# Deformable convolution and attention on one core: one transfer for a tile's places, and row maxima by way of DRAM

## The chip, the cores and the metric

The kernel runs on one core of a Trainium2 chip. The metric is the device time of one execution in microseconds. Three runs of the kernel before took 3164.89, 3168.13 and 3178.74 us; their median is 3168.13 us.

## What is computed

The input x is 8 images of 56 x 56 places with 128 channels, float32. Layer 0 is a block with a deformable 3 x 3 convolution, layer 1 causal attention over the 3136 places of an image and an expert layer in which each expert takes 8 places of each image.

```python
xp = x @ w_in + b_in
h = gelu(batch_norm(depthwise_conv3x3(x)))
offset, mask = h @ w_off + b_off, softmax(h @ w_msk + b_msk)   # 4 groups, 9 taps each
y = dcn_core(xp, offset, mask) @ w_out + b_out
x = x + gamma1 * layer_norm(y)
x = x + gamma2 * layer_norm(gelu(x @ w_fc1 + b_fc1) @ w_fc2 + b_fc2)
t = t + attention(norm(t))          # causal, softmax(q k / sqrt(T)) v, T = 3136
t = t + experts(norm(t))            # 64 experts, the 8 places of an image with the highest gate
```

`dcn_core` reads xp, padded by one place with zeros on each side, at nine shifted positions by bilinear interpolation. As long as no offset exceeds one place, each output place depends on the 5 x 5 places around it, and the interpolation becomes a sum over 25 taps with weights by place and group; places outside the image count as zero.

## The kernel before, in words

The work is cut into 32 groups: 8 images b with 4 groups s each. A group has one or two chunks of 448 places (8 rows of 56), that is 448 or 896 places, in tiles of up to 128: 200 tiles in all (`sizes`, `tiles`, lines 45 to 60).

For each group there are generators, each a step in the list `ORDER` (one letter a step, written out by hand or by a planner ahead of time): the program is laid down in exactly that order, and every engine works its own instructions off in the order in which they stand. A `need(...)` names an engine, an assumed duration, a buffer that is taken or given back, and from when; these figures do nothing in the program, they are what the order was planned with.

- `prepare` (L487): loads a chunk of x, transposes it on PE (L497), stores the transposed chunk to DRAM for later (`xTd`, L504), multiplies by `w_in` (L516) and stores the result into an image in DRAM (`img`, L529), in two transfers of 56 partitions. There are two such images, used in turn. An image has rows of `IW` = 60 places: 56 and two zero places on either side, with two zero rows above and below; the zeros are written once at the start (L347 to L354).
- `conv` (L538) and `plan` (L569): the depthwise convolution on DVE (L554), then offsets and masks, and from them on POOL the tap weights `taps` [128 places, tile, 5, 5 x 4 groups] (L631 to L645).
- `fetch` (L653): for each tile of 128 places, SP brings for each place its 5 x 5 x 128 values, 5 pieces of 640 values, into a buffer `g` of 3200 values a partition; three buffers exist. As a row of the image is 60 long and only 56 count, a tile's places are taken row by row of the image: 3 or 4 transfers with 8 to 56 partitions, 616 in all (L667).
- `weigh` (L673): DVE multiplies `g` by the weights (L692). `sums` (L697): POOL adds up the 25 parts in six additions (L708 to L718) into `ys`, after which the buffer is free for the next fetch.
- `project` (L778): output projection, norms and the two matrix products of the block on PE (L798, L812, L824), with norms on ACT, POOL and DVE.
- `norm` (L879): normalised places `z`, transposed `zT`, and the queries `qT`. Row 0 of `qT` is later used for the largest score, as `zT` holds a row of ones there.
- `scores` (L917) and `maxes` (L937): PE computes the scores of a tile of queries (L924), DVE takes the largest of each query (L947, L949) into `neg` [128 queries, tile], negated. The queries lie across partitions there, so at the end of a group PE transposes each column of `neg` into one row (L959, 224 in all) and ACT copies it into row 0 of `qT` (L966, 56 in all).
- `keyed` (L986), `exps` (L1006), `attend` (L1017): PE computes the scores once more with the keys across partitions and with the maxima already subtracted by row 0 (L993), ACT takes exponentials (L1014), PE multiplies by the values (L1025).
- `after` (L1040): residual, gate and the choice of the 8 places; at the end the experts' weights are loaded and the expert layer runs (`weights`, `hidden`, `share`).

The row that the change is about, and the fetch:

```python
for u in range(N // CH):                       # in maxes, L952
    pr = gen(f"pr{nm}_{u}")
    ...
    nc.tensor.transpose(pr[:1, ...], neg[r : r + w, i : i + 1], ident[r : r + w, r : r + w])
    ...
    nc.scalar.copy(qT[:1, u * CH : (u + 1) * CH], pr[:1, :CH])
while t < t0 + n:                              # in fetch, L662
    h0, w0 = divmod(t, HW)
    w = min(HW - w0, t0 + n - t)
    src = bass.AP(src.tensor, src.offset, [[C, w], [IW * C, 5], [1, 5 * C]])
    nc.sync.dma_start(g[t - t0 : t - t0 + w].rearrange("p (r f) -> p r f", r=5), src)
    t += w
```

SP issues the loads of x, the fetches, the loads of `xTd` and the weights, all in one queue in the order of `ORDER`; ACT issues the stores in its own.

Of the kernel before, what the change touches and what calls it, by code (L numbers as in the profile page):

```python
# [8 lines left out]
F32 = mybir.dt.float32  # L9
# [45 lines left out]
def tokens(b, s):  # L55
    return CH * sizes(b)[s]
# [18 lines left out]
def need(engine, us, take=None, give=None, since=None, kind=None, when=None, lock=False):  # L75
# [27 lines left out]
    "pppppppkbbpppwpwbpwwwppwpvkffvfvvvvvvvwvpbwpwccpcccpwcwcccppbccpcccwpcwpcpccvcwvcvcvcvcvcvcv"  # L103
    "cvwggvvvsvvwvwwvwvvsvgvpbpscsspsccsfpgppbpspcpscpscvscvssfvvcvcvcvcsvvcvscscsvcvcvcvvcvsvcfv"
    "cvcgvpbvpcccpvcvpvppbcvpcvcvsgpvgcsvccvscvvssvsvsfmvmpmvpvmvsvgvpbmpsmpscssmpsfmppbmpgmmpsmm"
    "pmmcsmpsmsvscvsfvcgcmscmcvgcsmcscsmsmsfvmkvmnnnnncsvnvvgsnnsnsnsnfcncgnnqcqqcqcxxcxxxcxctcte"
    "ctetaegaecaaccscagooccvsooovoosooscovvvsovsosfovovovovocosvpbopcsopscospsosfoppbpgcpsccosccs"
    "scsspfmpmvmgsmmvvsmvvssmsmsfmgmmsmmmmmsmsvvsssfmgmsmvvgmsmsmskmssfmgmmmmcmsmmsmcmmscmmscmgmm"
    "mscfcccmmcmcmcmcmkmnncnncnnncngcnsnnnccvcncvnvsnvnvgnsvnvnsnvsnsvsfvnvnpnbpqsqxqxqqsqsqsssfc"
    "xcxxxcqxccqxcqxcqqxqxxsqxqxqxsqxspxsgsxfmxmxxmtpstcptgvteetestmtacsaveavemaegsamsasttesfemea"  # L110
    "atmtaemceasvmmvvtsmvmsvtmsmssfamemgstvsmttgsmaeaesaessfaemgaamtctestmeaemakmcaammosmocmoscgm"
    "smcsmcfmomcmmcoocommocmmoomoomoocomccogomcoosmomomoccmokcsmvnnvnngsnnonnossovnovvovsonsfnvnv"
    "nvnnvnconsvononscponbpnsoossnsfvnvpnvcqpqxspvpqbxpqxqsxqxosqxsqcsxfxcmqmgqccqqmxsxqmxqxxqxqx"
    "sqcxqsxqxqsxsqxqsxmqfxcqmqxxqxqxqxcqcmqmcxcmxqxmmcxgcxmmcxpcmxmxpstmgtpmesvvsvamvtvtgessmtet"
    "esmtsftagaemeasmtemstkmasmesamssafemeamgttmetsmttaaesmeamsemssamsfmagamtettseaeteamcamcmcamc"
    "aemsgcsacmtsctemcegstcmsfcetcvcmamacesmaktmstcnncntsncnstncsntnscfaecepcabpagtnpeeetsntpntnt"
    "cnasnaecansnasesengsfanaeenanampnasmpnobpnosmncomcqoqxcoqocqxmxqxqxsqmxsqxssfmxqmqxomxqomocm"
    "oxcopgmmsqmmqcmpqcxpqxcvxqcxqvqxcqxocqgcqsmssxgssfxxxqmvqxqxmoqoqmxoqxqxxqsoxmoxqomoqsqxoxom"
    "sxoqksgosqmsfomqmmxqmxqsxqxqxmxqxqsxmqxsoxsmosqmsfoxmogqmmomsmoqmxmsxomvxsmvxsovssfvvxvxgctv"
    "stetstcvagsvtesvesavesfaevmavtoteooomttsectmgasmeasaesaesmafcvcmcakvcctgctmsemstmteevstcvpcs"  # L120
    "tbscmscpfsnannanenpnnnaeasgetmtstestpstaspsfpeabptagaepeseaaeaspatapststvsevtnfevaevgaemangn"
    "anstnntntnvenvtncvencaevnasveamagctsnesanssnsfmntmqeqxqxqxccqxcqxqcxacxcmcqmmxccqcmmsxgcmmst"
    "mstssccgsfmvccvevvcesvcavmavstvcmtvetvesmtstssfetcmgcaaecaesaevamacscpsqbpctsctsexpcfctpetge"
    "tpctcvtacaecvmevakvaecvaecmvcaaxamcxvomvxmoxctcmvocgtemteamatemeoaatmteameommoaoooaomomootmo"
    "motmemoootmtaomteoamomemoaomokmssonmonnmsnonenmsnonseosanofmoaaomnosmooommnonsmonnnosnmonsms"
    "gosnsfmmncnmnogmcnsonomoconosomvcvcsvscsvcsfvqvmoqxqxqxcmoqcqxsmqxqxcxqocxqxqcqsoxoxmsoxqsom"
    "sqofxomxqkmcomqcmqcomoxcqxmcxqxqxomxqovcmoxcvqocmxocmqovmvqmcxmxcogcxmmvcpmmbxmcxvmgcxpcopmo"
    "tptmoeottetgetptmaaevmeamvemakmsssssnpesntonsfntnbnptnanavepevnavpaevasnavnttnvptsteesaetsae"
    "stnsfnagntntenansgnanensansenssansfeaqqxqxsqxqxqxgmsqmqssmsfqmxsaxxtxtegaesaqqmxqxqsmxsqxqxs"
    "mxsqsfmqxmxgqmmscmmsccmxmvscqscmsqgcfsxcqxqxcqxcgptcbsctptscmescesescfcxcqmcqgttqmaaecqexmcx"  # L130
    "acxaxacmapmopcmocqkmqspnnqnnqnxqxqxnqxxqxsnqxnqxnxnqsxnxmsngpsmnbspsmfonxopxmxpsoqooqxoxcpqx"
    "cqovxqxoqcxqocqxomtxoxtesomtcagoeteqeqsoqsoxqsoxsfoqxoxqoqxoxoqxoqxgsvqxqvosvmoamssovsmvsofv"
    "amvavmxoxmmsgqomosmosqmsqossmfoxxxoosgtmqqseqmqxsxmqsxqsxstfxxtegcexvmsaavmaxsvgmvtkmscstesc"
    "tcfsvtcvtcveacgemamsemamsavtemvctvcstmcsctsecfacetcegtavcacacetctceaecpecmbpacmatcamepcmcmpc"
    "tgmmtmpmtmepmbpamaaemamtpeempampamtkmssvmesvtmvtsevtessvtsfvtvmvavaesaeaesaemasasstmftetsema"
    "gaetaesttetsetgmstmsasmesfagaeaeammsttamnosenntosasenosnensfmotmnonmaomngaeatsnaentoonstonoo"
    "tnosnotsonsaesfegcenanenanscgcnvcscacasvtscvstvsftvemevevnvcovvccgncsanoaoasoqoqcsmtsxxstcft"
    "omgetoaeeqeqvqxxqqmxqcacoomcaomcaxxmpkmxqcbgpcqocmoctmoxepcmcpoxcpocxvaovxovcxovtcxotceoaoot"
    "etvemavavemvtavemtatemeamatameommommotmomootomaoeomooaemtttemetmoaaameamemakmssonmnanmnonmsn"
    "onnosmostssftoetteoaoaeomaooonemonmannmonamnonnogcmnmonommnsccnmncvcmsnvcnomvcvmovovocosvsnv"  # L140
    "sqsfmvqvqxqvxqxoxpmqxbcoqxsmqxqxcomsxqcmgsqpsxqsxsqfovxqxmxpkmompqsmpmxopmscqbqxscqpsqxsmfxq"
    "xqxmqccmqmcxmcxqmxmocpxmcoxomcxgomxcomxomctcmoecgctmctctepcetgpmtaaeaevaevmavtvmetmvtemvtkms"
    "sssstvasnasefnnaennnaenanamomantotevtesnoaoenoaonsoaonotnsoonstonsesfnganentnnetsngneanoaaqs"
    "ooqxsoqxsosoqxsfoqxqoxoqxoqxoxtsogotsoesqeqsqxsxqsfxqxqxqxoxmosgomqqosmqxqsxmqxssxqsxfmxqmax"
    "mgamsmcmsmcgcsomsmvsctsfmcopeombgpsopsmqcspqsxqcmcxqxqcsxcfqxcqxmcqxqxpqcmtmtxexmetckmsssstc"
    "asagecaesacfaqqcaqxsqxqxxqxoxmcnxomspxmbnpgxcosxpmststnsnentmfeotenmgaoaseananmptnngopnocton"
    "otoeoenocootnceqmovgaaesoaoaoqosxoqxosvqosxoqsxosfqvqxqxoxmxovocmvcmvqvmqxsovqxqxcqvsqxoxmso"
    "xsgomsmsfotmqeqxqxsoqqxsxqoxqsooqssqsfxmxxgcqcmcsxqvcqmxcqxsmqxcasxvsxmcstmsfxvmxtvkmvtcevtc"
    "vstecvtevctsgcacsaegsmesamfaemecamgaamttteemaataemveamvacmcpcmmbtgcmcpmctctmmccpmcemcpcececp"
    "pabmaapmttepemapapmtvvtemtevmetvkmsssssvtsvtsfvtvavaetestaaesaesaesasesfattegttstaeaesaeaesg"  # L150
    "asasmasfmntnoennoamnnsnomntotsetgestestsftnoaoaeomgnaeaesnamttoeomnootseonotonansmnaesmesgas"
    "msfmcmnccnmvcocvnavnmnvsvanvonsvmnvosqqmvsqgvsqsfvgmooooosoxoxpxqbpsxqxqscmqxqxxqxcmptxspmst"
    "gftemetetpamvaevaevcavcvacvocmvtkocmocemoacmcoxogcmxcxmotxmtovtecvetcoetmcotocomamaectectaca"
    "ecaeaeaacmacmocmommommotomoomoooetmtttemaetmteomamemtkmssonmnoanamnnsonmennostesaostmnfoaaom"
    "eoetsoamoaooaemeanmansanmonosnonsnsmmngscsfnomnnccnvosgmncocmnsomncsocqososoqxsfqmxqxoqxqcgm"
    "cscvcsxxqsmvsqxsqfoomqoqxomxqxqxoxmoqmoqxomoxqxkmqxocmqmcomxoqcmxqcqomxqxcomxqcxomxqmocxmcvo"
    "xmcvmxvcmxvmxvomcmvtcmvtcgvmcvececgamcatmtoemovavometmomeakmssopooabmpsntnnstnsmnpnesseftptn"
    "pnptbpvmvnaveaevmavsavtteeansateantsesaesnasfgnantnntetemageasmnpnsmpnamnspsnsmnsfnmgmtnmqse"
    "qxqxsqxqsxqsxqsxsfqxqxqxqxqxsaxgmqsmmsqsmqsxsfmxxgscmqccmxqcqvsmcqcsxqcsxsqxsfxqcxmcxpcmqbcm"
    "xpqkscqxcmtsgtxectesctegctcttaaesasegsfaeaeaamqmqacnmsnnnonmqxnxqxoqsnqnxsnqxmqnxqxsmxqsxsfq"  # L160
    "xmxqmqgnmsnnpnsxmoxcqosxcqxpsoxcoqxxpxqxsqsfxqoxqqxxqoxmxcoqmocomxcoqmcoomqgcqcqcompmbpxxgxs"
    "oxogopmsqqomqpqxpsqxsvsxqmsxfqxqxoxoqxoqxosqvoxmomqosxmvoksmxsvmostvsfmoevtvtmgoeomsaaemoqva"
    "sxmqvstostesoootsftegaeceavsaacgscmvtxsmtesctsvsftveaveavecgaccasctctesteccmseacsmcmsvacfvmm"
    "cvamvcmcgtmcvcpmbpcccecpcmacpcxtpmtettgeeaaeatmtxpatbpatepeemptmptmtkmsssssssfvavaevtesvtasa"
    "etesvvvvsmvsasfaeaeaemttsgettstassgaesaesfaeaeagasttetseaeststeassfaeaatamnennnsomnnanntmtoe"
    "tengmoaaesnanstnosntsegtsfneoaenanmcmgsomccomsoomcsoaosvonosotvsfnvmmnvmmngtmotetmsovececosv"
    "oovsonvsasvcnfcgnctntctceacqecaqexacoxqecoqoxcqovcxqvqxqcxqxmcxqxpxabpmgacampcotopctecoctocm"
    "eomeaocmokmcomcamoptotovetetvotvvmvamvavaemveavmttetaemexmamexamaaxamxommotmmomtoemoooooeoam"
    "atmtteeaoamtatoemomtemoakmssonmnoannmsonenmnsonesomsanfaotomntetoooaseoeamnmnaomnanmsnnmmong"
    "csnmmsnsnsmmnsfcgcnmncvcmncvscvvvscvqmovqxoqqxcxoqvcqxcmqxxqsmxqsxsqxsfqxmxqvmqxmsqkxmvmqoxm"  # L170
    "cvmoxpcqboqmxcqxpqmxqcqmsxqxcvqxosxmsqxsmpcfxmooxmomcocooxcommxcommoxomtgcoetcmcecovvacmpacv"
    "ocpvpmvtbvtevmtoaeegmopaattmevmtkomssssssemsftnmgpettmasmpannoanseoenteompnaonaeosantmstosan"
# [2153 lines left out]
```

## Time and profile before

| | us |
|---|---|
| median of three runs | 3168.13 |
| profiled execution, device time | 3183.68 |
| its span in the trace | 3181.9 |
| TensorE (PE) busy | 2810.6 |
| GpSimd (POOL) busy | 2292.4 |
| VectorE (DVE) busy | 2210.9 |
| ScalarE (ACT) busy | 1629.2 |
| mean granted clock of PE | 0.94 of full |

In the trace's rows an instruction stands with its line, its engine, what it writes and reads (`g<-img` writes g from img), how many there were, their busy time in all, the mean duration in ns, and the idle time of the engine before them with what ended it. "PEld" is the loading of weights into TensorE, which goes beside matmuls. Each float32 matmul shows as two. The chain is followed back from the last instruction: at each step to what released it. A name ending in q is an engine's sequencer.

### The profile page before, as it was taken

Reading aid. Unit: us, or ns where it says so; the run is one execution under the profiler, and the core shown is the slowest. Engines: PE = TensorE matmul, PEld = TensorE weight load, DVE = VectorE, ACT = ScalarE, POOL = GpSimd, SP = SyncE. Lnnn points to the kernel's source line nnn. Section 1 sums busy time; section 2 is a strip of 40 time slices with the busy share of each in tenths; the row PEclk is TensorE's granted clock in tenths of the full one; section 3 lists DMA queues with packets and bytes.
Section 4 is the critical chain, followed back from the end, with each engine's and each line's share of the span. In section 5 each row is a group of like instructions: output and inputs, shape, how many; then the busy total and the mean of one; then the engine's idle time right before and its main releaser. Section 6 shows DMA issues by size and latency. Waiting matters only on the chain.

```text
span 3181.9 us, 37170 instructions
## 1 busy us (share of the span) xinstructions
PE 2810.6 (88%) x11785; PEld 1620.5 (51%) x11785; DVE 2210.9 (69%) x3887; ACT 1629.2 (51%) x3791; POOL 2292.4 (72%) x2415
## 2 busy tenths in 40 slices
PE   3458899999999999999998999998999999999671
PEld 3334455555555555555555555554555555655331
DVE  6766769777866896678668786687577855466540
ACT  2334565564666456664565556653666455633210
POOL 3878898778876898688858878677568885523543
PEclk7568899999999999999999999999999999999786
DMA  6866778647773787477845867467554857130360
GB/s 167 168 152 147 159 154 180 151 110 168 174 163 80 166 176 160 104 154 170 173 104 112 191 159 168 99 145 155 108 128 100 191 128 148 34 135 12 119 223 26
DMA packets 279862, 442.35 MB, mean 139 GB/s; under 512 B 18977, under 2 KB 132921, under 8 KB 279657
## 3 DMA queue, kind: packets, MB, share of 16 engines
q1 hardware_dynamic: 189352, 382.34, 54.7%
q10 hardware_dynamic: 87040, 51.40, 5.9%
q0 software_dynamic: 3264, 6.15, 0.7%
q8 instruction: 95, 1.56, 0.2%
q14 instruction: 111, 0.90, 0.1%
HBM read 386.03 MB, written 53.95 MB: 138 GB/s over the span
## 4 chain that ended last, share of the span: by engine, by line
PE 57%; DVE 14%; DMA 12%; POOL 9%; ACT 3%; issue 3%; SPq 1%; another core or an unknown queue 1%; ACTq 0%; POOLq 0%; DVEq 0%
PE sc L924 13%; PE av L1025 11%; PE st L993 11%; DMA g<-img 9%; PE ph L812 4%; DVE g L692 4%; PE pm L824 4%; POOL g L708 2%; DVE pv L554 2%; DMA xTd<-xc 2%; POOL g L710 1%; DVE mx L947 1%; PE py L798 1%; PE pg L1097 1%; PE pc L1054 1%
## 5 line engine op out<-in xcount | busy, mean ns | idle before, releaser
L692 DVE TENSOR_TENSOR g<-g,tp 128x3200 f32<-128x3200 f32 (+1 forms) x200 | 696.1, 3482 | 267.4 <-DMA g<-img 184.5
L708 POOL TENSOR_TENSOR g<-g 128x1536 f32<-128x1536 f32 (+1 forms) x200 | 688.9, 3445 | 60.2 <-DVE g L692 53.3
L924 PE MATMUL sc<-zT,qT 128*128 128x512 f32 (+4 forms) x1594 | 625.5, 525 | 18.1 <-DVE mx L947 8.2
L993 PE MATMUL st<-qT,zT 128*128 128x448 f32 (+8 forms) x1606 | 630.5, 513 | 10.2 <-ACT pe L1014 3.9
L1025 PE MATMUL av<-pe,zk 128*128 128x448 f32 (+8 forms) x1606 | 625.1, 513 | 16.3 <-ACT pe L1014 12.8
L1014 ACT ACTIVATE pe<-st 128x448 f32<-128x448 f32 (+8 forms) x803 | 392.1, 504 | 367.0 <-PE av L1025 175.6
L947 DVE TENSOR_REDUCE mx<-sc 128x1 f32<-128x512 f32 (+6 forms) x797 | 439.8, 583 | 97.4 <-PE sc L924 81.4
L924 PEld LDWEIGHTS sc<-zT,qT 128*128 128x128 f32 x1594 | 274.0, 188 | 266.2 <-issue 116.2
L1025 PEld LDWEIGHTS av<-pe,zk 128*128 128x128 f32 (+1 forms) x1606 | 286.3, 192 | 240.2 <-issue 166.2
L993 PEld LDWEIGHTS st<-qT,zT 128*128 128x128 f32 (+1 forms) x1606 | 278.1, 191 | 225.8 <-issue 155.9
L710 POOL TENSOR_TENSOR g<-g 128x768 f32<-128x768 f32 (+1 forms) x200 | 363.5, 1818 | 10.9
L554 DVE SCALAR_TENSOR_TENSOR pv<-xg,dw,pv 128x448 f32<-128x448 f32 x448 | 307.4, 686 | 31.0 <-ACT pv L551 19.8
L812 PE MATMUL ph<-xT,fc 128*128 128x512 f32 (+2 forms) x448 | 221.7, 586 | 24.9 <-DVE xT L754 21.8
L816 ACT ACTIVATE hid<-ph,b_fc 128x512 f32<-128x512 f32 (+2 forms) x224 | 140.8, 634 | 149.1 <-PE ph L812 146.8
L712 POOL TENSOR_TENSOR g<-g 128x384 f32<-128x384 f32 (+1 forms) x200 | 201.4, 1007 | 12.1
L645 POOL TENSOR_TENSOR taps<-taps,a 128x252 f32<-128x252 f32 (+1 forms) x288 | 190.5, 661 | 18.8
L635 POOL TENSOR_TENSOR a<-w 128x756 f32<-128x756 f32 (+1 forms) x96 | 135.8, 1415 | 86.2 <-DVE w L626 77.0
L824 PE MATMUL pm<-fc,hid 128*128 128x128 f32 x1600 | 194.7, 280 | 0.0
L824 PEld LDWEIGHTS pm<-fc,hid 128*128 128x128 f32 x1600 | 184.1, 193 | 11.6 <-issue 11.4
L1231 POOL TENSOR_TENSOR share<-share,part 128x512 f32<-128x512 f32 x56 | 71.0, 1268 | 130.8 <-DVE part L1221 114.0
L742 POOL TENSOR_SCALAR ssb<-ssb 128x4 f32<-128x4 f32 (+1 forms) x56 | 11.7, 208 | 176.3 <-ACT sqb L740 175.8
L812 PEld LDWEIGHTS ph<-xT,fc 128*128 128x128 f32 x448 | 78.4, 200 | 90.3 <-issue 41.1
(259 smaller groups left out, 4213.0 us busy)
## 6 DMA issues: line engine op xcount, KB each, us to landing
g<-img SPq DMA_DIRECT2D x280, 700.0 KB
g<-img SPq DMA_DIRECT2D x56, 600.0 KB
g<-img SPq DMA_DIRECT2D x56, 500.0 KB
g<-img SPq DMA_DIRECT2D x56, 400.0 KB
g<-img SPq DMA_DIRECT2D x56, 300.0 KB
w1t<-in_L_ffn_weight_dram SPq DMA_DIRECT2D x32, 512.0 KB
w2t<-in_L_ffn_weight_dram SPq DMA_DIRECT2D x32, 512.0 KB
xin<-in_x_dram SPq DMA_DIRECT2D x56, 224.0 KB
```

The costliest lines, as they stand in the source:

```text
L554: nc.vector.scalar_tensor_tensor(p3, src, dw[:, k : k + 1], p3, op0=ALU.mult, op1=ALU.add)
L692: nc.vector.tensor_mul(g3, g3, tp[:n, lt % 4].unsqueeze(2).to_broadcast([n, NTAP * NG, 32]))
L708: nc.gpsimd.tensor_add(g[:n, : 12 * C], g[:n, : 12 * C], g[:n, 12 * C : 24 * C])
L710: nc.gpsimd.tensor_add(g[:n, : 6 * C], g[:n, : 6 * C], g[:n, 6 * C : 12 * C])
L712: nc.gpsimd.tensor_add(g[:n, : 3 * C], g[:n, : 3 * C], g[:n, 3 * C : 6 * C])
L812: nc.tensor.matmul(ph[:, :n], fc1[:, f * P : (f + 1) * P], xT[:, :n], start=True, stop=True)
L824: nc.tensor.matmul(four(pm, m)[:, i, :], hid[:, f, i * P : (i + 1) * P], fc2[:, f, :], start=False, stop=i == m - 1 and f == 3,)
L924: nc.tensor.matmul(pp[:w, :n], qT[:, i * P : i * P + w], zTs[b, g][:, k0 : k0 + n], start=True, stop=not diagonal,)
L947: nc.vector.tensor_reduce(mx[:w, i, j : j + 1], pp[:w, :n], AX.X, ALU.max)
L993: nc.tensor.matmul(pp[:w, :n], zTs[b, g][:, j * P : j * P + w], qT[:, u * CH + q0 : (u + 1) * CH], start=True, stop=m <= 0,)
L1014: nc.scalar.activation(pe[:w, :n], pp[:w, :n], AF.Exp, scale=SCALE)
L1025: nc.tensor.matmul(av[:, q0:CH], zs[b, g][:w, j, :], pe[:w, : CH - q0], start=first, stop=last)
```

## The change

Three things are edited, and the order is written anew.

1. The image in DRAM loses its side borders: rows are 56 places long, with two places ahead of all and two behind. A tile's 128 places then stand 512 bytes apart throughout, across ends of rows, and `fetch` is one transfer of 128 (or 64) partitions x 5 x 640 values for each tile. A place near a side now reads places of the row above or below in the columns that lie outside.
2. These columns are masked: a constant `inside` [128, 7, 20], made from the column of each place, is 0 where a tap lies outside, and `plan` multiplies `taps` by it on POOL, once for each group. The columns come from an input that the general path already had.
3. `maxes` no longer transposes `neg`. ACT stores it to a row in DRAM (two such rows in turn), one value at a time; SP loads the row, of up to 896 values, into row 0 of `qT`. For a group of 448 places the store takes two transfers.

`ORDER` is another list of the same steps, planned with other figures for `need`, and a few small buffers share a tag.

```diff
-    imgs = [indram(f"img{j}", [IW * IW, C]) for j in range(2)]
+    imgs = [indram(f"img{j}", [IW * HW + 4, C]) for j in range(2)]
+    rows_ = [indram(f"maxes{j}", [GT * P]) for j in range(2)]
...
+    column = cst.tile([P, GT, 2], F32, tag="column", name="column")
+    nc.sync.dma_start(column, pos[:, :GT, :])
+    inside = cst.tile([P, GT, 5 * NG], F32, tag="inside", name="inside")
+    nc.vector.memset(inside, 1.0)
+    for k, limit, op in ((0, 2.5, ALU.is_gt), (1, 1.5, ALU.is_gt), (3, 55.5, ALU.is_lt), (4, 54.5, ALU.is_lt)):
+        nc.vector.tensor_scalar(
+            inside[:, :, k * NG : (k + 1) * NG],
+            column[:, :, 0:1].to_broadcast([P, GT, NG]),
...
     for im in imgs:
-        ahead, behind = 2 * IW + 2, (HW + 2) * IW + 2
+        ahead, behind = 2 * HW + 2, 2 + (HW + 2) * HW
         nc.sync.dma_start(im[:ahead, :], zero[:ahead, :C])
-        nc.sync.dma_start(im[behind:, :], zero[: IW * IW - behind, :C])
-        edge = im[ahead + HW : ahead + HW + 1, :]
-        nc.sync.dma_start(
-            bass.AP(edge.tensor, edge.offset, [[IW * C, HW], [1, 4 * C]]), zero[:HW, :]
-        )
+        nc.sync.dma_start(im[behind:, :], zero[:ahead, :C])
...
+        yield need(POOL, 0.18 + 0.22 * nt)
+        nc.gpsimd.tensor_mul(
+            taps[:, :nt],
+            taps[:, :nt],
+            inside[:, :nt].unsqueeze(2).to_broadcast([P, nt, 5, 5 * NG]),
+        )
         plans[b, s] = taps
...
-            at = yield need(SP, 0.5, take="g", since=None if lt == 0 else 0.0)
+            at = yield need(SP, 6.2 * n / P, take="g", since=None if lt == 0 else 0.0)
             g = sp.tile([P, NTAP * C], F32, tag="g", name=f"g{b}_{s}_{lt}", bufs=GB)
-            t = t0
-            while t < t0 + n:
-                h0, w0 = divmod(t, HW)
-                w = min(HW - w0, t0 + n - t)
-                src = im[h0 * IW + w0 : h0 * IW + w0 + 1, :]
-                src = bass.AP(src.tensor, src.offset, [[C, w], [IW * C, 5], [1, 5 * C]])
-                nc.sync.dma_start(g[t - t0 : t - t0 + w].rearrange("p (r f) -> p r f", r=5), src)
-                t += w
+            src = im[t0 : t0 + 1, :]
+            src = bass.AP(src.tensor, src.offset, [[C, n], [HW * C, 5], [1, 5 * C]])
+            nc.sync.dma_start(g[:n].rearrange("p (r f) -> p r f", r=5), src)
...
-        for u in range(N // CH):
-            yield need(PE, 0.45, take="gen")
-            pr = gen(f"pr{nm}_{u}")
...
-                nc.tensor.transpose(
-                    pr[:1, o - u * CH : o - u * CH + w],
-                    neg[r : r + w, i : i + 1],
-                    ident[r : r + w, r : r + w],
-                )
-                o += w
-            yield need(ACT, 0.52, give="gen")
-            nc.scalar.copy(qT[:1, u * CH : (u + 1) * CH], pr[:1, :CH])
+        at = yield need(ACT, 0.45)
+        full, part = N // P, N % P
+        row = rows_[(NGRP * b + s) % 2]
+        nc.scalar.dma_start(
+            row[: full * P].rearrange("(i p) -> p i", p=P), neg[:, :full]
+        )
+        if part:
+            nc.scalar.dma_start(row[full * P : N].rearrange("(p i) -> p i", i=1), neg[:part, full : full + 1])
+        at = yield need(SP, 0.1, since=at + 4.0)
+        nc.sync.dma_start(qT[:1, :N], row[:N].rearrange("(o n) -> o n", o=1))
+        yield need(DVE, 0.0, since=at + 2.6)
```

## The prediction

> **What bounds the kernel now.** I read the page's busy line first, then the busy time by stretch, then the chain that ended last.
>
> ```profile
> PE 2810.6 (88%) x11785; PEld 1620.5 (51%) x11785; DVE 2210.9 (69%) x3887; ACT 1629.2 (51%) x3791; POOL 2292.4 (72%) x2415
> ```
> ```profile
> 0.00:400.00 400.00, 241.70 (x952) 154.66 (x953) 281.83 (x431) 159.21 (x365) 294.83 (x348) 0.75 0.72 158
> 400.00:2760.00 2360.00, 2265.90 (x9249) 1304.91 (x9248) 1725.76 (x2921) 1365.90 (x3195) 1843.70 (x1909) 0.99 0.66 143
> 2760.00:3182.00 422.00, 303.00 (x1588) 160.96 (x1586) 203.29 (x536) 104.07 (x231) 153.85 (x159) 0.86 0.28 97
> ```
>
> The second fence gives, after stretch and length, the busy time of PE, PEld, DVE, ACT and POOL, then clock, DMA share and GB/s. PE is idle for 158 us in the first 400 us, for 94 us in the 2360 us of the middle (4%) and for 119 us at the end. The middle is TensorE's: there only two things pay, less PE work and fewer of these 94 us. The beginning has room for everything that delays PE.
>
> ```profile
> PE 57%; DVE 14%; DMA 12%; POOL 9%; ACT 3%; issue 3%; SPq 1%; another core or an unknown queue 1%; ACTq 0%; POOLq 0%; DVEq 0%
> ```
> ```profile
> by line: DMA g<-img 19.7%; PE sc L924 10.0%; PE ph L812 8.3%; POOL g L708 6.8%; DVE g L692 5.2%; PE pm L824 4.6%; POOL g L710 3.7%; issue 3.0%; POOL taps L645 2.9%; POOL g L712 2.5%; PE py L798 2.4%; DVE pv L554 1.6%; PE st L993 1.6%; POOL
> ```
> ```profile
> DVE g L692 <- DMA g<-img: 184.5, 65, 9.7
> ```
>
> The last two are the chain of 200 to 400 us by line and the longest wait between engines. The largest thing on the chain that isn't PE is the fetch of the places: 9% of the whole span (8.8% in the chain's own view, 280 us), 19.7% of 200 to 400 us.
>
> How fast that fetch is shows where one tile is fetched alone, and beside it a stretch in which weights arrive on all 128 partitions in packets of 2048 B:
>
> ```profile
> DMA packets 717, 1.72 MB, mean 166 GB/s; under 512 B 44, under 2 KB 44, under 8 KB 717
> q1 hardware_dynamic: 717, 1.72, 82.1%
> ```
> ```profile
> DMA packets 4003, 7.75 MB, mean 387 GB/s; under 512 B 231, under 2 KB 231, under 8 KB 4001
> q1 hardware_dynamic: 4001, 7.72, 104.3%
> ```
>
> The first stretch is 2037.2 to 2047.6 us, about 10.4 us for 640 packets of 2560 B (1.64 MB); the engines count as 82% busy and move 166 GB/s. The second moves 387 GB/s with busy engines. So in the fetch a packet takes twice as long for its bytes: 0.821 x 16 x 10.4 / 640 = 0.21 us against 16 x 20 / 3770 = 0.085 us for 2048 B, which would be 0.106 us for 2560 B.
>
> **What the Trainium skill says.** "DMA: Bandwidth & Descriptors", section "Why a DMA increments its semaphore by 16 and not by 1": a transfer runs on the largest k up to 16 that divides its slowest dimension. A row of 56 places gets 14 engines, 40 gets 10, 24 gets 12, 8 gets 8; 128 or 64 get 16. The trace agrees on ACT's queue: q10 has 87040 packets, and its data are 83200 (images 112 x 224, transposed chunks 56 x 128, outputs 50176, constants 768). The other 3840 are 142 x 16 + 112 x 14, the completions of 142 transfers on 16 engines and of the 112 image stores of 56 partitions on 14.
> "SBUF — State Buffer", section "Door 1: The DMA port swizzle": partitions p and p+32 share a port, so pieces of 56 partitions make engines meet on ports, while a transfer of 128 gives each engine its own. The 0.21 us against 0.106 us agree; that the ports are the cause isn't shown.
> "DMA: Bandwidth & Descriptors", section "Queues, rings and completion order": a queue's ring is taken in order, and an engine alternates between queues packet by packet. So a row read on SP's queue stands behind fetched places, and a store on ACT's is slowed by them. The trace agrees in kind: stores on ACT's queue (img<-st) stand on the chain with 7.50 us at 121.78 us and 10.41 us at 728.32 us.
>
> **A: the largest scores leave PE and ACT.** The transposes L959 go, and the copies L966:
>
> ```profile
> 0.00:3182.00 3182.00, 36.12 (x224) 15.92 (x224) 28.99 (x56) 0.94 0.62 139
> ```
>
> That is 36 us of PE and 29 us of ACT for the tile pr; the 14 us of idle time before their weight loads go in part. On the bound engine this counts in full: between -36 and -50, I take -40. ACT issues 32 + 8 = 40 stores at about 0.34 us (as L529) instead; at 51% busy neither moves the end.
>
> **B: a tile's places in one transfer.** 616 transfers become 200. SP saves 416 issues at 0.37 us, about 1.2 us of first-to-last issue in each tile; SP itself isn't the bound. The data take 1.64 MB / 387 GB/s = 4.2 us at best; were the packets to stay slow, only the balance would gain: the busiest engine of 56+56+16 has 45 packets, in the one transfer 40, so 9 us of data become 8. I take 387 GB/s, as the shape is the same 128 partitions: issue, first byte and completion (about 1.8 us) with it make 6 us instead of 10.4, 42% less. Of the chain's 280 us that is 118 us, but the PE's idle time caps it. In the first 400 us the chain has 47 us of fetch (5.7% of 60 to 200 us, 19.7% of 200 to 400 us), so 20 us go. In the middle it has 231 us (11.5% of 400 to 1000 us, 10.2% of the next 1000 us, 7.9% of 2000 to 2760 us), and 42% is 97, more than the 94 us that PE idles there; what is late next is POOL (78% busy in that stage) and the mx and ACT steps, so I take 35. Together -55; bounds 0 (hidden) and -118.
>
> **C: no side borders.** Two of six zero stores go (the chain has 6.04 us of img<-zero at 9.60 us), one small load and five small DVE operations come: -2, bounds -5 and +3.
>
> **D: the mask.** One product on POOL for each of 32 groups over up to 700 elements. L635 with 756 elements takes 1563 ns, L710 with 768 takes 1818: 1.55 us, and 1.0 for the 8 short groups (L712): 24 x 1.55 + 8 = 45 us. Behind it on POOL stand the sums of a tile (L708 on), which free the buffers for the next fetch. POOL has 9% of the span on the chain for 72% busy, an eighth: +6. If POOL were the bound it would be +45.
>
> **E: the new way of the row.** Keyed scores (L993) of a group now wait for a store on ACT, a wait on SP, and a load on SP. Queued behind ACT's issue is little; behind SP's wait stand the next fetches and loads of x. The trace has no 4-byte store. The store lies between 2.2 us (the page's time to landing of out_dram<-rows) and the 10.4 us above; I take 4, as the fetches will leave the engines freer. The load lies between 2 and 6 (estimates: as short as that store, or behind a fetched tile of 6 us); I take 2.5. With the last reduction (0.7) and two issues (0.7) the way takes 7.9 us. What covers it is the PE work that the changed program's order puts between a group's last score and its first keyed score, counted at 0.00168 us a column (L924: 0.86 us for 512): 12 of 32 groups have 0.1 to 8.8 us there, 6.7 on average; one has 10.0; the others have 12.4 to 61. So 12 x 1.2 = 15 us, and with scatter +20. At the upper ends the way takes 17.8 us: 12 x 11.1 and some 19 us of five others, +150. It isn't below 0: nothing is taken off that way but A.
>
> **Sum.** -40 - 55 - 2 + 6 + 20 = -71. Against the profiled execution (3183.7 us; its span 3181.9) that is 3113; the median of the runs is 15.6 us lower, so 3168 - 71 = 3097 us. The whole order of instructions is rewritten as well; every term carries that uncertainty.
>
> **The rivals.**
> B+: the fetch was what kept PE idle: the middle keeps 30 of its 94 us and the beginning loses 60 us. -40 - 64 - 60 - 2 + 6 + 20 = -140: 3028 us. For it: 0.72 DMA share in the first 400 us at clock 0.75. Against: POOL is 74% busy there too.
> C-: packets stay slow or the fetch was hidden: B is 0, -40 - 2 + 6 + 20 = -16: 3152 us. For it: PE is 96% busy in the middle although DVE waits for places. Against: 387 GB/s on the same queue.
> D+: slower. SP becomes a link between POOL and PE: the row's load stands behind a fetch that waits for a free buffer, and the ACT store behind fetched packets. For it: the wait of SP for POOL's ys L718, 1233.1 us in 161 waits, the longest 26.4; 12 groups with under 9 us of cover. Against: the planned order puts the load between fetches. At E = 150 the sum is +59: 3227 us. It decides from E = 91, that is 12 x 7.6 us, a way of 14.3 us.
>
> **How the numbers follow.** Forecast 0.56 (3050 to 3140), B+ 0.14, C- 0.16 (3140 to 3175), D+ 0.14. A measurement of this kernel can't tell less than about 0.5% (16 us) from no change. Faster by more: 0.56 + 0.14 + 0.05 of C- = 0.75; slower by more: 0.12 of D+; within: 0.11 + 0.02 = 0.13. The range runs from 3010, which cuts 0.04 off B+, to 3185, which leaves 0.12 of D+ out.
>
> **What would show it.** A: no pr, PE busy about 2770. B: about 6 us for a tile fetched alone, q1's share well under 54.7%, DVE's wait for g<-img below 100 us. D: 32 products of about 1.5 us on POOL. E: PE waits for qT<-maxes, in total about 20 us. The forecast is wrong if a tile takes 9 us, or if PE or its weight loads wait over 90 us for the row.

## The result and the profile after

Four runs of the changed kernel took 3211.33 to 3223.81 us, median 3218.03, beside 3168.35 for the kernel before: a ratio of 1.0144 (interval 1.0116 to 1.0172). Taken by the ratio the kernel is 46 us slower (0.0144 of 3168; the medians differ by 50), where 71 us less had been forecast. The time lies above the range; the slower rival D+ had named 3227 us. Of all executions in this document one, of the kernel without a store further down, was slow (9206.67 us at a granted clock of 0.398), and the ratios leave it out.

The profiled execution has a span of 3218.0 us. Its busy line, then its busy time by stretch in the columns that the prediction explains:

```profile
PE 2796.0 (87%) x11561; PEld 1625.1 (50%) x11561; DVE 2191.8 (68%) x3892; ACT 1613.1 (50%) x3743; POOL 2343.8 (73%) x2447
```
```profile
0.00:400.00 400.00, 244.55 (x964) 157.91 (x965) 287.06 (x440) 163.29 (x384) 320.06 (x371) 0.80 0.53 166
400.00:2760.00 2360.00, 2212.43 (x8873) 1284.47 (x8872) 1679.04 (x2861) 1326.48 (x3077) 1840.65 (x1889) 0.97 0.45 141
2760.00:3218.00 458.00, 339.04 (x1727) 182.72 (x1725) 225.69 (x593) 123.34 (x283) 183.06 (x189) 0.87 0.27 94
```

PE lost 224 instructions, as the change says, but only 14.6 us of busy time. Its idle time (span less busy) rose from 371 to 422 us, all of it in the middle: 148 us there where it was 94. That is the stretch which the prediction called TensorE's own, and the loss lies there. The chain that ended last says whose it is, by engine and by line:

```profile
PE 63%; POOL 12%; DMA 11%; DVE 8%; issue 2%; ACT 2%; ACTq 0%; SPq 0%; POOLq 0%; DVEq 0%
PE st L1000 15%; PE av L1032 14%; PE sc L935 14%; DMA g<-img 5%; DMA maxes<-neg 5%; PE pm L835 4%; PE ph L823 4%; POOL g L719 3%; DVE g L703 2%; POOL g L721 2%; PE pg L1104 1%; PE py L809 1%; DMA qT<-maxes 1%; PE pqq L907 1%; DVE mx L958 1%
```

DMA has 11% of the chain where it had 12%, but with other contents: the fetch fell from 9% to 5%, and the store of the largest scores takes 5% that no line of before had. Four of the chain's waits for it, with the load that follows (start, length, what; all in us):

```profile
277.85 9.27 DMA maxes<-neg
287.25 3.79 DMA qT<-maxes
...
1868.95 12.62 DMA maxes<-neg
...
2454.03 9.69 DMA maxes<-neg
2463.86 3.67 DMA qT<-maxes
...
2881.27 9.99 DMA maxes<-neg
```

From the issue of the store to the issue of the load the 32 groups take 9.2 to 21.9 us, median 11.4, where the prediction took 4. Who waits, from the list of waits (us in total, times, longest):

```profile
DVE g L703 <- DMA g<-img: 132.2, 38, 10.7
...
PE st L1000 <- DMA qT<-maxes: 99.6, 14, 22.6
...
PEld st L1000 <- DMA qT<-maxes: 47.4, 8, 8.3
```

PE waits for the row in 14 of the 32 groups. The 8 waits of its weight loads fall into groups among these 14, as the weights come from the same row: they are the same time seen twice, and the two lines must not be added (the 147 us of some expectations below is that sum; the wait is 99.6 us). DVE still waits 132 us for places, although a full tile now takes about 6 us (median 6.2 from issue to the last byte; before, a tile fetched alone took 10.4). The waits for the row, and about half of the wait for places, turn out to have one cause, and one stretch shows it best: the last of the four stores above, with nothing else under way. It is 11.8 us long, in 40 slices of 0.295 us: busy tenths of the DMA engines, then the packets and the queue.

```profile
DMA  0004714000000000000000000000000000000000
...
DMA packets 913, 0.02 MB, mean 2 GB/s; under 512 B 912, under 2 KB 912, under 8 KB 912
...
q10 hardware_dynamic: 912, 0.00, 3.5%
```

The 896 values of 4 bytes and the 16 completions are all recorded as done in the first 2.1 us. Yet the load is let go only 10.1 us after the store was issued. The engines look idle while the completion (the signal that lets the waiter go on) is outstanding; packet records alone would have given a store of 2 us.

### The profile page after: what moved, and what is told of

Its sections match the earlier page's. It is cut to its first block, busy times and chain, and to the rows that moved or that the text cites. A ratio compares the mean times of both kernels' runs of the same rounds, so it can differ in the third digit from the quotient of the medians.

```text
span 3218.0 us, 36068 instructions
## 1 busy us (share of the span) xinstructions
PE 2796.0 (87%) x11561; PEld 1625.1 (50%) x11561; DVE 2191.8 (68%) x3892; ACT 1613.1 (50%) x3743; POOL 2343.8 (73%) x2447
## 4 chain that ended last, share of the span: by engine, by line
PE 63%; POOL 12%; DMA 11%; DVE 8%; issue 2%; ACT 2%; ACTq 0%; SPq 0%; POOLq 0%; DVEq 0%
PE st L1000 15%; PE av L1032 14%; PE sc L935 14%; DMA g<-img 5%; DMA maxes<-neg 5%; PE pm L835 4%; PE ph L823 4%; POOL g L719 3%; DVE g L703 2%; POOL g L721 2%; PE pg L1104 1%; PE py L809 1%; DMA qT<-maxes 1%; PE pqq L907 1%; DVE mx L958 1%
## 5 line engine op out<-in xcount | busy, mean ns | idle before, releaser
L703 DVE TENSOR_TENSOR g<-g,tp 128x3200 f32<-128x3200 f32 (+1 forms) x200 | 695.0, 3479 | 155.0 <-DMA g<-img 132.2
L1000 PE MATMUL st<-qT,zT 128*128 128x448 f32 (+8 forms) x1606 | 650.8, 528 | 100.8 <-DMA qT<-maxes 99.6
L1000 PEld LDWEIGHTS st<-qT,zT 128*128 128x128 f32 (+1 forms) x1606 | 287.5, 197 | 330.3 <-issue 222.7
L721 POOL TENSOR_TENSOR g<-g 128x768 f32<-128x768 f32 (+1 forms) x200 | 364.1, 1820 | 10.6
L765 DVE SCALAR_TENSOR_TENSOR xT<-ptb,c_L_conv_ln_g,xT 128x512 f32<-128x512 f32 (+2 forms) x56 | 38.2, 681 | 143.9 <-PE ptb L763 143.6
```

The costliest lines, as they stand in the source:

```text
L703: nc.vector.tensor_mul(g3, g3, tp[:n, lt % 4].unsqueeze(2).to_broadcast([n, NTAP * NG, 32]))
L721: nc.gpsimd.tensor_add(g[:n, : 6 * C], g[:n, : 6 * C], g[:n, 6 * C : 12 * C])
L1000: nc.tensor.matmul(pp[:w, :n], zTs[b, g][:, j * P : j * P + w], qT[:, u * CH + q0 : (u + 1) * CH], start=True, stop=m <= 0,)
```

## The experiments

Twelve kernels were run, each three rounds beside the kernel before on its chip; that kernel took 3187, 3172 and 3186 us in the three batches, so ratios are compared.

**Each part by itself.** First the fetch, the borders and the mask in the order of before, with the transposes on PE and the copies on ACT kept:

```diff
-    imgs = [indram(f"img{j}", [IW * IW, C]) for j in range(2)]
+    imgs = [indram(f"img{j}", [IW * HW + 4, C]) for j in range(2)]
...
+            inside[:, :nt].unsqueeze(2).to_broadcast([P, nt, 5, 5 * NG]),
...
-                nc.sync.dma_start(g[t - t0 : t - t0 + w].rearrange("p (r f) -> p r f", r=5), src)
...
+            nc.sync.dma_start(g[:n].rearrange("p (r f) -> p r f", r=5), src)
```

> The kernel before with the one transfer a tile, the image without side borders and the mask, in the order of before, with transposes for the row. S with the forecast's terms B, C and D: -55 - 2 + 6, about 3117 us. R: the fetch is hidden or the mask costs its 45 us: 3165 to 3210 us.

Measured: 3093.6 us, ratio 0.9708 (0.9675 to 0.9741), that is -92 us against the median shown. The middle and the fetch's wait:

```profile
400.00:2760.00 2360.00, 2312.13 (x9545) 1343.99 (x9544) 1771.70 (x3057) 1390.44 (x3256) 1881.28 (x1942) 0.99 0.43 146
```
```profile
DVE g L702 <- DMA g<-img: 29.5, 12, 7.7
```

PE idles 48 us in the middle where it did 94, and DVE's wait fell from 184.5 to 29.5 us. The fetch does what it was meant to, and more than forecast.

The same in the changed kernel's order, by giving it back the transposes and copies:

```diff
-            row[: full * P].rearrange("(i p) -> p i", p=P), neg[:, :full]
...
-        nc.sync.dma_start(qT[:1, :N], row[:N].rearrange("(o n) -> o n", o=1))
...
+                nc.tensor.transpose(
+                    pr[:1, o - u * CH : o - u * CH + w],
+                    neg[r : r + w, i : i + 1],
...
+            nc.scalar.copy(qT[:1, u * CH : (u + 1) * CH], pr[:1, :CH])
```

> The changed kernel with the maxima put into the row by PE transposes and ACT copies again; fetch, mask and the new order stay. Theory S (the one-value stores to DRAM complete only after some 11 us, and PE waits for the row): PE's 147 us of waiting for the row go, 36 us of transposes come back, about 3218 - 147 + 36 = 3107 us. Rival R (the new order, the mask on POOL or the fetch itself cost the time): 3180 us or more.

Measured: 3094.28 us, ratio 0.9709 (0.9676 to 0.9742), the same within the intervals. With the transposes kept, the rewritten order is worth nothing that can be measured, for good or ill.

The row alone, put into the kernel before, its load at the next place of SP in that order:

```diff
-            nc.scalar.copy(qT[:1, u * CH : (u + 1) * CH], pr[:1, :CH])
...
+            row[: full * P].rearrange("(i p) -> p i", p=P), neg[:, :full]
...
+        nc.sync.dma_start(qT[:1, :N], row[:N].rearrange("(o n) -> o n", o=1))
```

> The kernel before with the row by way of DRAM alone, in the order of before. S: a way of about 14.5 us against the 0.5 to 13.9 us of PE work that the order of before has there in 18 groups, about 150 us of waiting, less 36 us of transposes: about 3280 us. R: within 20 us of 3168.

Measured: 3445.31 us, ratio 1.0808 (1.0763 to 1.0852), +256 us, more than either theory said.

```profile
DVE g L693 <- DMA g<-img: 269.1, 64, 13.0
...
PE st L990 <- DMA qT<-maxes: 235.1, 23, 16.3
...
PEld st L990 <- DMA qT<-maxes: 32.7, 4, 10.1
```

Besides PE's wait for the row, DVE's wait for places went up by 85 us, although the fetch wasn't touched. So the row costs the fetch something too, by its traffic or by SP's wait ahead of the load; this run doesn't tell which.

**What of the row costs it.** My theory was that each small packet of the store takes about 10 ns in turn, as 912 of them need some 10 us. Longer pieces: the row is laid out by query partition, so that each partition writes its 7 values as 28 contiguous bytes, and the load picks single values instead.

```diff
-            row[: full * P].rearrange("(i p) -> p i", p=P), neg[:, :full]
+            row[: full * P].rearrange("(p i) -> p i", p=P), neg[:, :full]
...
-        nc.sync.dma_start(qT[:1, :N], row[:N].rearrange("(o n) -> o n", o=1))
+        nc.sync.dma_start(
+            qT[:1, : full * P].rearrange("o (i p) -> o i p", p=P),
+            row[: full * P].rearrange("(o p i) -> o i p", o=1, i=full),
+        )
...
```

> The changed kernel with the row laid out in DRAM by partition: the store of a group of 896 is 128 pieces of 28 bytes instead of 896 of 4, and the load picks single values. Theory S1 (each small piece written to DRAM costs some 10 ns of completion, 896 of them 9 us): store 3 us, load some 4 us, PE's waiting for the row nearly gone, 3070 to 3110 us. Rival S2 (a small store to DRAM completes after some 10 us however many pieces it has): as the changed kernel, 3200 us or more. If single values are as slow to load as to store, also 3200 us.

Measured: 3083.09 us, ratio 0.9728 (0.9694 to 0.9762). Store and load on its chain:

```profile
270.85 3.04 DMA maxes<-neg
274.03 6.49 DMA qT<-maxes
```

The store fell to 3 us. The load rose to 6.5 and takes part of it back, but the kernel is now faster than before. That fits the count of packets; it doesn't prove it. One thing in this run speaks against it: in the 8 short groups the last 64 values are still stored one by one, and although they are few, SP waits for them after the pieces are there:

```profile
SPq L977 <- DMA maxes<-neg: 33.3, 8, 6.8
```

By the completions in the trace these 64 values take 7.7 us in the median, the stores of pieces 2.3.

A store for each tile as soon as its largest scores are there, 128 values each:

```diff
+                nc.scalar.dma_start(
+                    row[i * P : i * P + w].rearrange("(p i) -> p i", i=1), neg[:w, i : i + 1]
+                )
...
-            row[: full * P].rearrange("(i p) -> p i", p=P), neg[:, :full]
```

> The changed kernel with the store made tile by tile, each as soon as its 128 maxima are there (200 stores on ACT instead of 40). S1: only the last 128 values are still to complete when the group ends, a way of some 6 us in place of 14: little waiting left, but 160 more issues on ACT at 0.47 us, 75 us of its queue: 3090 to 3150 us. S2: 3200 us or more.

Measured: 3386.3 us, ratio 1.0695 (1.0652 to 1.0738), the opposite of what I expected. On its chain a store of 128 values can take as long as one of 896:

```profile
1492.13 8.45 DMA maxes<-neg
...
1968.43 15.12 DMA maxes<-neg
```

From a group's last store to the load the 32 groups take 8.5 us in the median, where the changed kernel takes 11.4 with up to seven times the values.

And the whole store made twice, first into a spare row:

```diff
+            spare[: full * P].rearrange("(i p) -> p i", p=P), neg[:, :full]
...
             row[: full * P].rearrange("(i p) -> p i", p=P), neg[:, :full]
```

> The changed kernel with the store made twice, first into a row that nobody reads. S1: 1792 pieces complete after some 20 us, 9 us more for at least 14 groups and some more groups without cover: 3350 us or more. S2: both complete side by side, within 20 us of the changed kernel's 3218 us.

Measured: 3191.38 us, ratio 1.0068 (1.0036 to 1.01), with stores of 10 to 11 us still:

```profile
1395.69 10.73 DMA maxes<-neg
...
2420.80 10.80 DMA maxes<-neg
```

From the second store to the load it is 11.0 us in the median. So a seventh of the packets takes 8.5 us and twice the packets 11.0, beside 11.4: the time doesn't follow the count, and the count theory falls. (By ratio this kernel is even 24 us faster than the changed one, and PE waits 68.1 us for the row instead of 99.6. No run says why, so a difference of that size can arise between two of these kernels without a cause that was found.)

What these two kernels have in common with the changed one is the distance between values: neighbours in DRAM, 4 bytes apart, come from neighbouring partitions as separate packets. New theory: writes that fall into the same small stretch of DRAM wait for one another, different stretches go in parallel. Three kernels space the values out; the number of values, the issue of the store and the order stay as in the changed kernel, and the load then picks single values. With a step of S values:

```diff
-    rows_ = [indram(f"maxes{j}", [GT * P]) for j in range(2)]
+    rows_ = [indram(f"maxes{j}", [GT * P, S]) for j in range(2)]
...
-            row[: full * P].rearrange("(i p) -> p i", p=P), neg[:, :full]
+            row[: full * P, 0:1].rearrange("(i p) o -> p i o", p=P), neg[:, :full].unsqueeze(2)
...
-        nc.sync.dma_start(qT[:1, :N], row[:N].rearrange("(o n) -> o n", o=1))
+        nc.sync.dma_start(qT[:1, :N].unsqueeze(2), row[:N, 0:1].rearrange("(o n) i -> o n i", o=1))
```

S = 16 (64 bytes):

> The changed kernel with its row laid out one value to 64 bytes: the same number of 4-byte values is stored by the same instruction, and the load picks single values. Theory (neighbours wait for one another: values written into the same 64 bytes of DRAM go one after the other, some 0.6 us each): the store's completion falls from 10 to 12 us to some 3 us, the load takes some 6 us as it did with the longer pieces, PE's waits for the row fall from 147 us to 40 to 60, and the time comes to 3080 to 3120 us. Rival (any 4-byte write to DRAM is slow, however far apart): the store stays at 9 to 12 us, the load is at 6, so the row's way grows, and the time is 3220 to 3280.

S = 128 (512 bytes):

> As the run before with one value to 512 bytes. Theory with 64 bytes as the place that values share: nothing more to gain, the store at 3 us and the time within 15 us of that run. Rival (the place that they share is of 512 bytes): the store falls to 3 us only here, and one value to 64 bytes still takes 5 us or more. Second rival (4-byte writes are slow alone): 9 to 12 us here too.

S = 2 (8 bytes):

> As the two runs before with a step of 8 bytes: eight values share 64 bytes where sixteen do in the changed kernel. Theory: half the neighbours, half the queue, so a store of 5 to 7 us, between the two; with a load of 6 us the time is 3150 to 3220. Rival (4-byte writes are slow alone): 9 to 12 us, time 3220 to 3280.

| step in DRAM | store issue to load issue, median (lower, upper quarter) | time, us | ratio (interval) |
|---|---|---|---|
| 4 bytes (changed kernel) | 11.4 us (10.6, 12.4) | 3218.03 | 1.0144 (1.0116 to 1.0172) |
| 8 bytes | 5.0 us (4.4, 6.4) | 3148.34 | 0.9882 (0.9857 to 0.9908) |
| 64 bytes | 3.2 us (2.5, 4.7) | 3101.37 | 0.9729 (0.9707 to 0.9751) |
| 512 bytes | 3.5 us (2.7, 4.4) | 3102.53 | 0.9731 (0.9707 to 0.9755) |

At 64 bytes, on the chain and in the waits:

```profile
265.38 3.58 DMA maxes<-neg
269.10 6.29 DMA qT<-maxes
```
```profile
PE st L1000 <- DMA qT<-maxes: 36.4, 13, 10.6
...
PEld st L1000 <- DMA qT<-maxes: 15.0, 8, 4.4
```

The same 896 values of 4 bytes, from the same place in the program, complete in less than a third of the time once they are apart, and the kernel goes from 46 us slower to 86 us faster (ratio 0.9729 of 3168) although its load has grown from about 4 to about 6 us. Neither the number nor the size of the packets is the cause; the neighbourhood in DRAM is. 64 and 512 bytes don't differ, so the stretch that is shared is, as far as these times tell, at most 64 bytes; 8 bytes is too little. The pieces of 28 bytes adjoin as well, two or three to 64 bytes, and take no longer (2.9 us by the same measure): what hurts is many writers to one stretch. Where between 8 and 64 bytes it ends, and what the memory does there, no run shows.

**The harm to others.** The row loaded from zeros written at the start, so that nobody awaits the store, which stays; the largest scores are then not subtracted:

```diff
-        nc.sync.dma_start(qT[:1, :N], row[:N].rearrange("(o n) -> o n", o=1))
+        nc.sync.dma_start(qT[:1, :N], still[:N].rearrange("(o n) -> o n", o=1))
```

> The changed kernel, store as it is, but the row is loaded from zeros written at the start instead of from the group's maxima: the largest scores are not subtracted before the exponential. S (waiting for the store to complete is what costs, on PE and in SP's queue, not the store's traffic nor the load): 3218 - 147 or less, 3050 to 3090 us, below the version with transposes. R (traffic of single values, or the load itself): 3150 us or more.

Measured: 3125.65 us, ratio 0.9857 (0.9822 to 0.9892), well above what I had expected. Then the same with the store left out as well:

```diff
-        nc.scalar.dma_start(
-            row[: full * P].rearrange("(i p) -> p i", p=P), neg[:, :full]
-        )
...
```

> Each group's store is left out and the load takes a row of zeros written once at the start, so the largest scores are not subtracted; PE transposes nothing and ACT copies no row. Theory (the store's traffic holds up the tiles' fetches even where nobody awaits it): the 32 us by which the run with an unawaited store lay above the kernel with transposes go, and what the transposes cost comes on top: 3040 to 3075 us. Rival (the load and its place in SP's queue are what costs): 3110 to 3130 as with the store.

Measured: 3064.92 us, ratio 0.961 (0.9582 to 0.9638). Waits with the store that nobody awaits, then without any:

```profile
DVE g L705 <- DMA g<-img: 123.4, 36, 9.4
...
PE st L1002 <- DMA qT<-still: 31.4, 4, 14.6
```
```profile
DVE g L705 <- DMA g<-img: 67.4, 29, 5.9
...
PE st L997 <- DMA qT<-still: 7.3, 1, 7.3
```

A store for which nothing waits costs 78 us (0.0247 of 3168, give or take 14 by the two intervals). DVE's wait for places shows 56 us of it, PE's for a row that was written long before 24. Call a store open from its issue to its last completion. The fetches of full tiles that overlap an open store in that kernel take 10.8 us in the median from issue to the last byte, the others 6.1; with a store for each tile it is about 12 against 6.1. With 64 bytes between the values it is 6.1 for those that overlap a store too, so it is not the company of just any store that slows a fetch. In the changed kernel one such stretch of 18 us, in slices of 0.45 us (busy tenths, then GB/s):

```profile
DMA  7040005990000293938009988248789999999999
GB/s 307 23 4 0 0 0 18 50 14 0 0 0 9 46 106 23 36 18 32 5 0 53 57 88 58 53 68 215 238 337 368 421 415 410 404 385 404 421 393 410
```

It shows the hold-up at work: the stores are issued 0.2 and 0.6 us into it, the next tile's fetch at 2.8 us, the row's load at 12.0 us. Between 2.8 and 12 us the engines are often counted as busy but move 0 to 106 GB/s; within 2 us of the store's completion they reach about 400. That tile took 13.9 us. But in the changed kernel only 21 fetches of full tiles overlap an open store. Sixteen of them were issued before it, and the median of all 21 is 6.2 us; the five that were issued while it was open take 13.9 to 19.2. SP, which waits for the store before it issues the row's load, keeps the next ones back (some of this wait lies before the stores are issued):

```profile
SPq L972 <- DMA maxes<-neg: 497.4, 33, 75.0
```

Of the 16 fetches that come next after a row's load in SP's queue, 15 are issued 0.3 to 0.4 us after it: they had been ready. Where SP waits for no store, the same 16 come 1.1 to 12.7 us after it.

**Another way round DRAM.** The columns of `neg` go from SBUF straight into row 0 of `qT`, one transfer of 128 single values a tile, issued by ACT:

```diff
+        for i in range(full):
+            nc.scalar.dma_start(qT[:1, i * P : (i + 1) * P], neg[:, i : i + 1])
```

> The changed kernel, but each column of maxima goes from its partitions straight into row 0 of the queries by a transfer of 128 single values on ACT's queue, without DRAM and without SP. S: no write to DRAM has to complete, a way of some 3 us, no waiting left to speak of: 3218 - 130 or about 3090 us, and lower than with transposes. R: 3200 us or more, as the number of single values is the same. If a transfer of single values is slow whatever it writes to, also about 3200 us.

Measured: 3153.31 us, ratio 0.9898 (0.9864 to 0.9933). PE waits for no row any more, but 192 issues at 0.56 us take 107 us of ACT's queue, and ACT itself now waits about 100 us for these transfers:

```profile
ACT hid L827 <- DMA qT<-neg: 24.7, 5, 9.0
...
ACT lg L1103 <- DMA qT<-neg: 16.1, 4, 4.7
...
ACT pe L1018 <- DMA qT<-neg: 15.0, 5, 4.0
```

**What is best.** Row by 64 bytes, row in longer pieces, and the new fetch with the old transposes: 0.9729, 0.9728, 0.9708 and 0.9709 (two orders). All beat both kernels, and their intervals overlap. So the new way of the row, even mended, is worth no more than the transposes; the gain of 2.7 to 2.9% is the fetch's.

## Why the prediction was wrong

In ratios of 3168 us, A to D without the store are 0.961 - 1 = -124 us (forecast -91), and the store and the wait for it are 1.0144 - 0.961 = +169 us (forecast +20 for E). By construction the two add up to the measured +46. The terms one by one:

- **A (forecast -40): right within the noise.** The kernel without store against the one with transposes in the same order: 0.961 - 0.9709, or -31 us (give or take 14 by the two intervals), its load still in it. PE's busy time goes from 2786.9 to 2757.0 us. In the changed kernel itself PE was 2796 instead of the forecast 2770, since the matmuls behind the row's wait are recorded longer: 650.8 us for st against 624.8 without the store. Whether that is the clock (0.934 against 0.955) or how an end is modelled isn't told apart.
- **B (forecast -55), C (-2), D (+6): right in kind, B too small.** Together -92 us (interval -82 to -103) against -51. A tile takes 6.2 us, as said. What the sum missed is that PE idle fell by 46 us in the middle, not 35 (and by 24 outside it, where 20 had been taken), and that its busy time fell by 26.6 us with the same instructions (2810.6 to 2784.0), which no step had. The granted clock of the two profiled executions is 0.940 and 0.950, which would be about that size; that it is the cause isn't shown. The rival B+ was nearer for this part. D's products are as priced:

```profile
L657 POOL TENSOR_TENSOR taps<-taps,inside 128x700 f32<-128x700 f32 x24 | 40.1, 1670 | 1.6
L657 POOL TENSOR_TENSOR taps<-taps,inside 128x400 f32<-128x400 f32 x8 | 8.3, 1035 | 0.6
```

  48.4 us, forecast 45. What of it lies on the path was not tried by itself; the whole came to -92 with it.
- **E (forecast +20): the step that failed.** The prediction took "4, as the fetches will leave the engines freer", between 2.2 and 10.4 us. The store takes 11.4, and it takes 10 on an otherwise idle DMA: it is hardly slowed by fetches, it slows them. With the load at about 4 us instead of 2.5 the way becomes 0.7 + 11.4 + 0.4 + 4 = 16.5 us. At that the prediction's own formula gives 12 x 9.8 = 118 us, and by estimate some 12 more from the groups with longer cover; PE waited 99.6 us in 14 groups, and awaiting the store costs 91 us by the runs (1.0144 - 0.9857). So formula and cover were right in kind, if somewhat high, and the input was wrong. What no step had is the harm to others: an unawaited store costs 78 us already. How the 169 us divide in the changed kernel itself isn't settled. Places come late there (DVE waits 132.2 us for them, 67.4 without store, 61.4 with transposes and 70.6 with a step of 64 bytes), mostly, it seems, because SP holds fetches back behind the row's load, and in some cases because the engines are held up.
- **D+, the slower rival,** came within 9 us of the time and named the right term and the point from which it decides. That closeness is in part luck: it took 33 us too little gain for A to D and 19 us too little loss for E (150 against 169), which largely cancel, and its 150 was all waiting, of which there was about 91. Its mechanism is half right at most. SP did become a link, but the other way round: fetches stand behind the row's load, which waits for the store. And the store isn't slow because fetched packets are ahead of it; it is slow alone, and fetched packets are held up by it.

The bound from 2.2 to 10.4 us was taken from stores of long rows. The nearest rows of the profile had the right size at the upper end, for another reason. The trace of before had no store of neighbouring 4-byte values, and the upper end then deserved more than the 0.14 that it got, as the sign of the whole sum hung on it from 14.3 us on.

Two places of the Trainium skill bear on it. "DMA: Bandwidth & Descriptors", section "Anatomy of one DMA — SWDGE (gpsimd) path", says of transfers that GpSimd issues that the completion waits until the last write is confirmed in the target memory, which can take surprisingly long for HBM. These stores are ACT's, so this is a likeness only; it agrees in kind with the store alone, packets done at 2.1 us and load let go at 10.1. The page puts most of a fixed cost of about 2 us there; the runs show 3 us for a whole store with values apart and 10 to 12 with neighbours. The section "Queues, rings and completion order", on which the prediction leaned, has an engine alternate between queues packet by packet. The stretch above shows that this doesn't protect a fetch: with both queues filled, it moved under 110 GB/s for 9 us.

## What to carry to other kernels

Before a handful of values takes the way through DRAM, ask not only how many bytes or packets that is but whether single values of different partitions land next to each other there: spread them by 64 bytes, or let each partition write a longer piece, and price the load that this makes longer. A DMA's end is where its waiter goes on, not where its last packet is recorded. And when the sign of a sum hangs on one unseen price, the upper end of that price is a case of its own.

## What the runs showed of the hardware

- Neighbouring 4-byte values written to DRAM by different partitions, from the store's issue to the load that waits for it: 11.4 us for 896 values, 11.0 for two such stores at once, 8.5 for a tile's 128 or 64. With the 896 values apart: 5.0 us at a step of 8 bytes, 3.2 at 64, 3.5 at 512; 2.9 us for adjoining pieces of 28 bytes.
- While a store of neighbours is open, fetches on another queue crawl: a tile's 1.64 MB takes 10.8 to about 12 us in the median instead of 6.1, and 13.9 to 19.2 where it was issued while the changed kernel's store was open.
- A load of 896 values that lie in one row onto one partition takes about 4 us, of values that lie apart about 6.
- The fetch by 128 partitions needs 118 ns on average for a packet of 2560 bytes, by 56 and fewer 193 ns.
